# A Mamba scan's spread products: one full-array product for each channel group instead of pairs of 32-row products

## The chip, the cores and the metric

The kernel runs on one core of a Trainium2 chip. The metric is the device time of one execution in microseconds, as the median of several runs. Engines have short names below: PE is TensorE (matrix products), DVE is VectorE, ACT is ScalarE, POOL is GpSimd and SP is SyncE, which issues transfers. Everything is float32, and every matrix product is issued as two passes, so that the profile counts two matmul records for one product in the code.

## The reference, cut to what matters

Two layers work on x of shape (4, 1024, 128): attention and a mixture of eight experts, then a Mamba block and a second mixture of experts. The change lies in the selective scan of the Mamba block:

```python
def _selective_scan(u, A, B_sel, C_sel, delta):
    deltaA = jnp.exp(delta[..., None, None] * A[None, None])
    deltaB_u = delta[..., None, None] * B_sel[:, :, None, :] * u[..., None]
    def step(h, inp):
        a_t, bu_t, c_t = inp
        h = a_t * h + bu_t
        y_t = jnp.einsum('bdn,bn->bd', h, c_t)
        return (h, y_t)
...
xz = x @ W_in
x_main, z = jnp.split(xz, 2, axis=-1)
... # depthwise convolution over 4 tokens
x_conv = jax.nn.silu(jnp.swapaxes(x_conv, 1, 2))
proj = x_conv @ W_xproj
B_sel = proj[..., :D_STATE]
C_sel = proj[..., D_STATE:2 * D_STATE]
delta = jax.nn.softplus(proj[..., -1])
A = -jnp.exp(log_A)
y = _selective_scan(x_conv, A, B_sel, C_sel, delta)
y = y + x_conv * D_param[None, None, :]
y = y * jax.nn.silu(z)
return y @ W_out
```

There are 128 channels (d), 16 states (n) for each, 4 sequences (b) and 1024 tokens in each.

## The kernel before

**Stages.** Attention with the first mixture of experts beside it fills the execution up to about 1425 us. Then the Mamba block runs, sequence by sequence, up to about 1965 us, with the last expert blocks of the first layer (`Blocks`, `first_blocks`), the preparation of the next sequence (`scan_inputs`) and the routing of the sequence before (`dispatch`) beside it. The second mixture of experts ends the program (`slots_steps`, `collect`, `last_experts`).

**The layout of the scan.** The 128 x 16 pairs of channel and state don't fit on 128 partitions, so the scan goes over 16 groups (NCH) of 8 channels; in a group the partitions hold 8 channels by 16 states. Tokens go in two halves of 512 (g). So there are 4 x 2 x 16 = 128 steps, taken two at a time by `scan(pair, g, ...)`.

**One step of the scan.** `du` (delta times the convolved input) lies with one channel on each partition. A product with a matrix of ones and zeros, `spread`, copies each of 8 rows of `du` to 16 partitions, into a PSUM bank `pu` (L909; one of four banks, `pu0` to `pu3`, in turn). DVE multiplies `pu` by B (L911). ACT makes `da`, the exponential of delta times A (L913). DVE runs the recurrence along the tokens (`tensor_tensor_scan`, L915), giving `h`; ACT keeps its last column as `carry` (L917); POOL multiplies by C (L919), giving `hc`. After four steps `collected` sums the 16 states of each channel by products with `gather`, each 32 columns wide and placed side by side in the array, into `py`, which the product of `skip` (D times the identity) has started.

**How `spread` is made and used.** `four` (L791) is the identity folded to 32 columns: every block of 32 partitions holds its own 32 x 32 identity. POOL widens each column 16 times (L793), so that `spread[:, v]` spreads the v-th 8 channels of each block of 32 rows. A product for group c takes only the 32 rows that hold its channels, `rows = 32 * (c // 4)`, and `spread[rows, c % 4]`. The two groups of a pair are chosen in the main loop so that their rows are in neighbouring blocks of 32. `next_to` keeps the second product of a pair right behind the first in the order on TensorE.

**Order.** Program order is written out by hand with generators (`Beside`, `take`): after each pair some steps of the work beside the scan are issued. A scheduler then orders the instructions of each engine; each engine works through its own list in order. A wait on one instruction holds up all that stand behind it on that engine.

**Other names that the prediction uses.** `p` are the products of `scan_inputs` (convolution with `conv_in`, `m_in`, `m_B`, `m_C`, and `ones` for the step sizes `dt`); `pd`, `pl`, `pin`, `fpl`, `fpin` and `pall` are products of few columns in the step sizes and the routing; `pw` is the output projection, whose gated result `wide_gated` (L936) POOL adds to x (L939); `tp` and `ftp` are transposes by the identity; `pf` are products of the first layer's experts; `hs`, `slots_in`, `xe` and `g_in` belong to the routing of the second layer; L195 is the last residual addition of attention.

Of the kernel before, what the change touches and what calls it, by code (L numbers as in the profile page):

```python
# [11 lines left out]
F32 = mybir.dt.float32  # L12
I32 = mybir.dt.int32
AF = mybir.ActivationFunctionType
ALU = mybir.AluOpType
AX = mybir.AxisListType
PSUM = bass.MemoryType.PSUM

P = 128
B, S, D = 4, 1024, 128  # L20
# [7 lines left out]
NST = 16  # L28
NCH = 16
# [15 lines left out]
def mm(nc, out, lhsT, rhs, start=True, stop=True):  # L45
    return nc.tensor.matmul(out, lhsT, rhs, start=start, stop=stop)  # L46
# [3 lines left out]
def adaln_two_layers(ctx: ExitStack, tc: tile.TileContext, I: dict, out: bass.AP):  # L50
    nc = tc.nc
# [16 lines left out]
    ident = cst.tile([P, P], F32, name="ident")  # L68
# [128 lines left out]
    def next_to(first, make):  # L197

        if first:
            make()  # L200
            return
        with tc.high_priority():
            tc.keep_in_program_order(make())
# [259 lines left out]
    with ExitStack() as es:  # L463
# [19 lines left out]
        for j in range(4):  # L483
            rows = slice(j * QG, (j + 1) * QG)
            nc.gpsimd.tensor_copy(mask[rows, MW - QG :], causal[rows, rows])

        for slots in f_in + xd + [g_in]:
            flat = slots.rearrange("(p r) d -> p (r d)", p=P)
            for at in range(0, flat.shape[1], 512):
                n = min(512, flat.shape[1] - at)  # L490
# [29 lines left out]
        def values(hT):  # L520

            v = ab.tile([P, TB, 4 * HD], F32, tag="v", bufs=1, name="v")
            for t in range(TB):
                pv = ps_m.tile([P, 4 * HD], F32, tag="m", name="pv")
                mm(nc, pv, hT[:, t * P : (t + 1) * P], wv)
                nc.scalar.copy(v[:, t, :], pv)
            return v
# [133 lines left out]
        for at, (b, c) in enumerate(stages):  # L661
            q, k = made
            if c == 0:
                v = values(hT)
# [72 lines left out]
    with ExitStack() as es:  # L737
        mc = es.enter_context(tc.tile_pool(name="mc", bufs=1))
        db = es.enter_context(tc.tile_pool(name="db", bufs=2))
        mb_scope = es.enter_context(ExitStack())  # L740
        mb = mb_scope.enter_context(tc.tile_pool(name="mb", bufs=2))
        fw_scope = ExitStack()
        fb = fw_scope.enter_context(tc.tile_pool(name="fb", bufs=2, side="right"))
        ps_u = es.enter_context(tc.tile_pool(name="ps_u", bufs=1, space=PSUM))
# [29 lines left out]
        def first_blocks(b):  # L774
# [12 lines left out]
        nc.scalar.activation(negA, m_logA, AF.Exp)  # L787
        nc.vector.tensor_scalar(negA, negA, -1.0, None, ALU.mult)

        four = mc.tile([P, 32], F32, name="four")  # L790
        nc.vector.tensor_reduce(four, ident.rearrange("p (r d) -> p d r", d=32), AX.X, ALU.add)  # L791
        spread = mc.tile([P, 4, 8, NST], F32, name="spread")
        nc.gpsimd.tensor_copy(  # L793
            spread.rearrange("p v a n -> p (v a) n"), four.unsqueeze(2).to_broadcast([P, 32, NST])
        )
        group = mc.tile([P, 8], F32, name="group")
        nc.vector.tensor_reduce(group, ident.rearrange("p (a n) -> p a n", n=NST), AX.X, ALU.add)
        gather = mc.tile([P, 4, 32], F32, name="gather")
# [10 lines left out]
        def wide(tag, bufs=2, cols=S):  # L809
            return mb.tile([P, cols], F32, tag=tag, name=tag, bufs=bufs)  # L810
# [85 lines left out]
        turn = itertools.count()  # L896

        def scan(pair, g, carry, dt, du, bb, cc):


            tok = slice(g * 512, (g + 1) * 512)
            hcs, pus = [], []
            for _ in pair:
                pus.append(ps_u.tile([P, 512], F32, tag=f"pu{next(turn) % 4}", name="pu"))
            for n in range(2):
                c = pair[n]
                rows = slice(32 * (c // 4), 32 * (c // 4) + 32)
                lhsT = spread[rows, c % 4].rearrange("p a n -> p (a n)")
                next_to(n == 0, lambda: mm(nc, pus[n], lhsT, du[rows, tok]))  # L909
            for c, pu in zip(pair, pus):  # L910
                nc.vector.tensor_mul(pu, pu, bb[:, tok])  # L911
                da = wide("da", 3, 512)
                nc.scalar.activation(da, dt[:, tok], AF.Exp, scale=negA[:, c : c + 1])  # L913
                h = wide("h", 3, 512)
                nc.vector.tensor_tensor_scan(h, da, pu, carry[:, c : c + 1] if g else 0.0, ALU.mult, ALU.add)  # L915
                if g == 0:
                    nc.scalar.copy(carry[:, c : c + 1], h[:, 511:512])  # L917
                hcs.append(wide("hc", 10, 512))
                nc.gpsimd.tensor_mul(hcs[-1], h, cc[:, tok])  # L919
            return hcs  # L920
# [8 lines left out]
        def scan_output(b, g, py, sz):  # L929

            y = wide("yh", 1, 512)
            nc.vector.tensor_mul(y, py, sz[:, g * 512 : (g + 1) * 512])
            pw = ps_m.tile([P, 4, D], F32, tag="d", name="pw")
            for q in range(4):
                mm(nc, pw[:, q], y[:, q * P : (q + 1) * P], m_out)
            u = mb.tile([P, 4, D], F32, tag="wide_gated", name="wide_gated")  # L936
            nc.vector.tensor_mul(u, pw, gate_a1[:, b : b + 1, :].to_broadcast([P, 4, D]))
            xt = x[:, b * TB + 4 * g : b * TB + 4 * g + 4, :]
            nc.gpsimd.tensor_add(xt, xt, u)  # L939
# [249 lines left out]
        for b in range(B):  # L1189
# [17 lines left out]
            for m in range(NCH):  # L1207

                g, n = divmod(m, NCH // 2)
                hcs += scan([4 * (2 * n % 4 + r) + n // 2 for r in range(2)], g, carry, *scanned)  # L1210
                for f in among:
                    if m >= f.at:
# [17 lines left out]
                if n == NCH // 2 - 1:  # L1230

                    def late(b=b, g=g, hcs=hcs, py=py, sz=sz):
                        collected(3, hcs, py)
                        scan_output(b, g, py, sz)

                    hcs = []
# [105 lines left out]
        _, placei, w = sent[0]  # L1342
# [74 lines left out]
```

## Time and profile before

| what | value |
|---|---|
| median of 3 runs | 2198.94 us (2198.32 to 2199.18) |
| profiled execution | 2186.78 us, span 2185.1 us |
| mean granted clock of TensorE, whole span | 0.878 |
| the same from 1470 to 1965 us | 0.66 |
| PE busy from 1470 to 1965 us | 384.80 of 495 us |
| DVE busy from 1470 to 1965 us | 361.39 of 495 us |
| products `pu` (two passes each) | 128, busy 146.5 us |
| scans `h` on DVE, 512 tokens each | 128, median 1.211 (first half) or 1.270 us (second) |

A page of the profile gives each engine's busy time, the span in 40 slices with tenths of busy time (and, in the row PEclk, tenths of the full clock that TensorE was granted), the chain of waits that ended last, and groups of instructions. A row of a stretch of time reads: the stretch, its length, then busy us and number of instructions of PE, of PE's weight loads, of DVE, ACT and POOL, then the granted clock, the share of the transfer engines and GB/s. A row of a wait reads: who waited, for whom, us in total, how many times, the longest. A row of the timeline reads: start, length, engine, line, operation, what it writes from what, shapes (for a product: rows * columns of the stationary operand, then the moving operand), and how many such records were merged.

### The profile page before, as it was taken

The page shows a single profiled execution, that of the slowest core. Times are in us where ns is not written, and L with a number is a line of the kernel's source. Part 1 is how long each engine was busy: PE and PEld are TensorE (multiplying, and loading weights), DVE is VectorE, ACT ScalarE, POOL GpSimd, SP SyncE. Part 2 cuts the span into 40 slices and gives each one's busy share as a digit, 9 for nine tenths or more (in the row PEclk, how much of TensorE's full clock was granted, in tenths as well). Part 3 has the DMA queues.
Part 4 walks back from the last instruction along what each step waited for, and adds up shares of the span by engine and source line. Part 5 has one row for each costly group of instructions (what it writes and reads, how often), then busy time and mean ns, then how long its engine had stood idle before and what let it go on. Part 6 is the DMA issues. An engine that isn't in the chain of part 4 may idle for free. (4 is left out here: it accounts for less than half of the span.)

```text
span 2185.1 us, 29044 instructions
## 1 busy us (share of the span) xinstructions
PE 1832.8 (84%) x8957; PEld 972.7 (45%) x8957; DVE 1321.1 (60%) x4001; ACT 939.5 (43%) x2067; POOL 993.6 (45%) x1277
## 2 busy tenths in 40 slices
PE   5399999998999898999988999959698858859784
PEld 3144444454555354455444456523245423227563
DVE  5446566565667755667675566537587785861323
ACT  1145454653454464445374455433564334323221
POOL 1334444346333736523644633244563666571524
PEclk9699999999999998999999999965687757559897
DMA  6300101002222101222200212110121220012425
GB/s 224 126 1 20 30 1 38 12 19 55 72 64 76 48 1 44 77 66 64 77 6 29 69 58 75 35 34 0 35 71 51 75 99 20 1 51 82 131 72 153
DMA packets 103756, 123.59 MB, mean 57 GB/s; under 512 B 15024, under 2 KB 68656, under 8 KB 103600
## 3 DMA queue, kind: packets, MB, share of 16 engines
q1 hardware_dynamic: 84256, 99.01, 15.4%
q0 software_dynamic: 8192, 16.74, 2.5%
q10 hardware_dynamic: 11152, 5.97, 0.9%
q8 instruction: 71, 1.16, 0.2%
q14 instruction: 85, 0.70, 0.1%
HBM read 67.85 MB, written 32.90 MB: 46 GB/s over the span
## 5 line engine op out<-in xcount | busy, mean ns | idle before, releaser
L586 POOL TENSOR_SCALAR pr<-pr,den 128x32 f32<-128x32 f32 (+31 forms) x512 | 353.2, 705 | 301.9 <-DVE den L583 295.8
L580 ACT ACTIVATE pr<-pr,nb 128x32 f32<-128x32 f32 (+31 forms) x512 | 371.6, 727 | 196.9 <-DVE nb L567 193.6
L595 PE MATMUL pt<-ident,pr 128*128 128x128 f32 x2304 | 341.9, 283 | 47.6 <-POOL pr L586 38.1
L46 PE MATMUL sc<-k,q 64*128 64x512 f32 (+14 forms) x1536 | 329.4, 520 | 43.8 <-DVE nb L567 25.3
L595 PEld LDWEIGHTS pt<-ident,pr 128*128 128x128 f32 x2304 | 253.2, 142 | 243.6 <-POOL pr L586 77.4
L46 PE MATMUL po<-pT,v 128*64 128x512 f32 x1152 | 344.7, 621 | 1.8 <-DVE pT L599 1.8
L597 ACT COPY pT<-pt 128x512 f32<-128x512 f32 x288 | 167.7, 582 | 354.9 <-PE pt L595 301.9
L567 DVE CUSTOM_DVE_ANT_0 pr<-sc,mask 128x512 f32<-128x512 f32 (+15 forms) x512 | 272.9, 559 | 73.5 <-PE sc L46 63.9
L599 DVE COPY pT<-pt 128x512 f32<-128x512 f32 x288 | 198.3, 688 | 167.2 <-PE pt L595 154.1
L919 POOL TENSOR_TENSOR hc<-h,cc 128x512 f32<-128x512 f32 x128 | 161.0, 1272 | 127.7 <-DVE h L915 60.2
L46 PEld LDWEIGHTS sc<-k,q 64*128 64x128 f32 x1536 | 122.4, 191 | 198.7 <-DVE nb L567 93.7
L46 PE MATMUL pu<-du,spread 32*128 32x512 f32 x256 | 146.5, 953 | 34.0 <-DVE h L915 30.1
L684 POOL MEMSET pr<- 128x288 f32 x128 | 42.3, 339 | 264.4 <-PE pt L595 260.3
L567 DVE CUSTOM_DVE_ANT_0 pr<-sc,mask,nb 128x416 f32<-128x416 f32 (+15 forms) x256 | 119.9, 496 | 7.0 <-PE sc L46 5.8
L913 ACT ACTIVATE da<-dt,negA 128x512 f32<-128x512 f32 x128 | 91.0, 718 | 75.8 <-DVE h L915 75.5
L911 DVE TENSOR_TENSOR pu<-pu,bb 128x512 f32<-128x512 f32 x128 | 85.9, 686 | 39.9 <-PE pu L46 39.4
L1302 POOL DMA_INDIRECT y<-slots_out,slot x56 | 57.9, 1033 | 108.4 <-PE ph L46 50.7
L46 PEld LDWEIGHTS po<-pT,v 128*64 128x64 f32 x1152 | 69.3, 135 | 84.1 <-issue 42.0
L503 DVE TENSOR_TENSOR rot_w<-proj,sin_sb 128x512 f32<-128x512 f32 x80 | 55.0, 688 | 77.5 <-PE proj L46 44.4
L46 PEld LDWEIGHTS pf<-fxT,fw 128*128 128x128 f32 x552 | 73.5, 202 | 53.6 <-DVE fye L450 15.5
L580 ACT ACTIVATION_READ_ACCUMULATOR pr<-pr,nb 128x1 f32 x512 | 96.3, 188 | 0.0
L545 POOL TENSOR_TENSOR q<-rot_u,rot_v 128x512 f32<-128x512 f32 x64 | 81.3, 1271 | 32.8 <-DMA rot_v<-rot_w 29.1
(273 smaller groups left out, 2714.3 us busy)
## 6 DMA issues: line engine op xcount, KB each, us to landing
fw<-in_f_w SPq DMA_DIRECT2D x92, 320.0 KB, 3.0
rot_v<-rot_w SPq DMA_DIRECT2D x320, 64.0 KB, 2.0
gw<-in_g_w SPq DMA_DIRECT2D x15, 512.0 KB, 5.2
fxe<-blocks_in SPq DMA_DIRECT2D x28, 192.0 KB, 2.6
blocks_out<-fye SPq DMA_DIRECT2D x28, 192.0 KB, 3.0
blocks_in<-mask SPq DMA_DIRECT2D x20, 256.0 KB, 5.2
slots_in<-mask SPq DMA_DIRECT2D x16, 256.0 KB, 4.7
g_w<-in_g_w SPq DMA_DIRECT2D x8, 512.0 KB, 6.4
```

Source lines behind the costliest of these rows:

```text
L46: return nc.tensor.matmul(out, lhsT, rhs, start=start, stop=stop)
L545: nc.gpsimd.tensor_add(to, u.rearrange("p (n q) -> p n q", q=QG), v.rearrange("p (n q) -> p n q", q=QG))
L567: nc.vector.tensor_tensor_reduce(out=pr[hp][:, g, lo:hi], in0=sc[:, hp, : hi - lo], in1=mask[:, MW - hi + lo :] if hi == nk else mask[:, : ...
L580: nc.scalar.activation(p, p, AF.Exp, bias=nb[:, last, hp : hp + 1], scale=-1.0, accum_out=den[:, hp : hp + 1])
L586: nc.gpsimd.tensor_scalar(p, p, den[:, hp : hp + 1], 1.0, ALU.mult, ALU.mult)
L595: next_to(hp == 0 and g == 0, lambda: nc.tensor.transpose(to, p, ident))
L597: nc.scalar.copy(pT[:, hp, :], pt)
L599: nc.vector.tensor_copy(pT[:, hp, :], pt)
L911: nc.vector.tensor_mul(pu, pu, bb[:, tok])
L913: nc.scalar.activation(da, dt[:, tok], AF.Exp, scale=negA[:, c : c + 1])
L919: nc.gpsimd.tensor_mul(hcs[-1], h, cc[:, tok])
L1302: nc.gpsimd.indirect_dma_start(out=y, out_offset=None, in_=yd[k][:, :], in_offset=bass.IndirectOffsetOnAxis(ap=slot[:, k, t : t + 1], axis=0),
```

## The change

`spread` gets one full 128-row operand for each of the 16 groups: POOL widens the whole identity, 128 columns to 128 x 16, so that `spread[:, c]` has ones where a row's channel belongs to group c and zeros in all other rows. The reduction into `four` goes. In `scan` each product takes all 128 rows of `du` and the operand of its group; the pairs' `next_to` goes, and a bank is taken right before its product. `spread` takes 8 KB of a partition where it took 2; `wide_gated` gets one buffer where it had two.

```diff
-        four = mc.tile([P, 32], F32, name="four")
-        nc.vector.tensor_reduce(four, ident.rearrange("p (r d) -> p d r", d=32), AX.X, ALU.add)
-        spread = mc.tile([P, 4, 8, NST], F32, name="spread")
+        spread = mc.tile([P, NCH, 8, NST], F32, name="spread")
         nc.gpsimd.tensor_copy(
-            spread.rearrange("p v a n -> p (v a) n"), four.unsqueeze(2).to_broadcast([P, 32, NST])
+            spread.rearrange("p c a n -> p (c a) n"), ident.unsqueeze(2).to_broadcast([P, P, NST])
         )
...
-            for _ in pair:
-                pus.append(ps_u.tile([P, 512], F32, tag=f"pu{next(turn) % 4}", name="pu"))
-            for n in range(2):
-                c = pair[n]
-                rows = slice(32 * (c // 4), 32 * (c // 4) + 32)
-                lhsT = spread[rows, c % 4].rearrange("p a n -> p (a n)")
-                next_to(n == 0, lambda: mm(nc, pus[n], lhsT, du[rows, tok]))
+            for c in pair:
+                pu = ps_u.tile([P, 512], F32, tag=f"pu{next(turn) % 4}", name="pu")
+                mm(nc, pu, spread[:, c].rearrange("p a n -> p (a n)"), du[:, tok])
+                pus.append(pu)
...
-            u = mb.tile([P, 4, D], F32, tag="wide_gated", name="wide_gated")
+            u = mb.tile([P, 4, D], F32, tag="wide_gated", bufs=1, name="wide_gated")
```

## The prediction

> **What bounds the kernel now.** I read the page first, then the tile query on `pu`, the waits of VectorE in the stretch where the scan runs, the PE timeline, and last that stretch cut into pieces of 3.41 us, because the granted clock turned out to be constant inside such pieces.
>
> ```profile
> span 2185.1 us, 29044 instructions
> PE 1832.8 (84%) x8957; PEld 972.7 (45%) x8957; DVE 1321.1 (60%) x4001; ACT 939.5 (43%) x2067; POOL 993.6 (45%) x1277
> PEclk9699999999999998999999999965687757559897
> L46 PE MATMUL pu<-du,spread x256: 587/1056/1218, 1470.9 to 1925.2; 32*128 32x512 f32 x128
> 1470.00:1965.00 495.00, 384.80 (x1250) 170.00 (x1249) 361.39 (x781) 199.82 (x378) 292.77 (x249) 0.66 0.14 44
> DVE pu L911 <- PE pu L46: 39.4, 17, 10.2
> DVE r_m L222 <- PE pl L46: 19.4, 5, 6.0
> DVE pos L975 <- PE pin L46: 11.0, 4, 4.9
> DVE wide_gated L937 <- PE pw L46: 8.9, 6, 3.7
> DVE yh L932 <- PE py L46: 5.5, 1, 5.5
> ```
>
> The clock row falls from 9 to between 5 and 8 in slices 27 to 36 (54.6 us each): that is the scan. All products that the change touches lie between 1470.9 and 1926 us. In 1470:1965 the columns are length, then busy time of PE, weight loads, DVE, ACT, POOL, then clock: PE works 384.8 of 495 us at a mean clock of 0.66, DVE 361.4. DVE is idle for 495 - 361.4 = 133.6 us, and the five waits shown, all on products of TensorE, make 84.2 us of that. So the stretch is held by two engines in turn: DVE, which has 128 multiplications (0.687 us) and 128 scans (1.21 or 1.27), 247 us in all, and a TensorE at half clock. The last 220 us (experts of the second layer) and the first 1425 hold no product of this kind.
>
> ```profile
> 1472.87 2.08 PE L46 MATMUL p<-xc,m_B_sb 128*128 128x512 f32 x2
> 1474.88 2.08 PE L46 MATMUL pu<-du,spread 32*128 32x512 f32 x4
> 1623.15 1.13 PE L46 MATMUL pu<-du,spread 32*128 32x512 f32 x4
> 1628.05 1.88 PE L46 MATMUL p<-hT,conv_in 128*128 128x512 f32 x4
> ```
>
> A product is two passes. At half clock a product on all 128 rows takes 2.08 us (x2), and a pair of 32-row products takes the same 2.08 (x4): the two run side by side. At full clock the pair takes 1.13 and two full-row products 1.88.
>
> ```profile
> 1472.62:1476.03 3.41, 3.41 (x8) 1.00 (x6) 2.92 (x4) 1.49 (x5) 0.00 (x0) 0.50 0.00 0
> 1510.17:1513.58 3.41, 3.41 (x10) 0.46 (x10) 3.39 (x7) 1.28 (x2) 1.99 (x2) 0.50 0.00 0
> 1513.58:1516.99 3.41, 3.25 (x8) 0.99 (x4) 3.41 (x11) 0.72 (x1) 1.67 (x2) 0.50 0.00 0
> 1540.89:1544.30 3.41, 3.41 (x5) 1.35 (x4) 3.41 (x11) 2.25 (x3) 3.24 (x3) 0.50 0.06 22
> 1544.30:1547.71 3.41, 3.41 (x16) 0.81 (x15) 0.23 (x3) 2.08 (x3) 3.22 (x4) 1.00 0.06 19
> 1776.41:1779.82 3.41, 3.41 (x14) 1.09 (x12) 3.41 (x1) 0.00 (x0) 3.41 (x2) 0.50 0.06 19
> 1779.82:1783.23 3.41, 0.46 (x4) 0.00 (x0) 3.41 (x2) 0.00 (x0) 3.24 (x2) 1.00 0.00 0
> ```
>
> PE is busy without a gap in nearly all of them, yet the clock comes up only after 1540.89 and 1776.41. I count passes by the part of the array that they use: 1 for 128 rows by 512 columns, a quarter for 32 rows, for a 32-column product of `gather` or for a 128-column transpose. 1540.89 held 4 passes of `conv_in`; 1776.41 one pass of `skip`, four transposes and eight of `gather`, also 4. 1472.62 held two full passes and four of `pu`: 3, and the clock stayed at 0.50. 1510.17 held eight of `gather` and one of `pu`: 2.25, and it stayed. So what raises the clock is array used, not time busy; about three and a half full passes in a piece are needed, and a 32-row product counts for little. Weights of ones and zeros (`gather`, the identity) count like others.
>
> **The change, part by part.** *Products.* 128 products of 32 rows, in pairs, become 128 of 128 rows, each alone. By start times, 80 of the 256 passes now run side by side at half clock (20 pairs), 80 at half clock without a partner, 80 in pairs at full clock (20 pairs) and 16 alone. A pass that has no partner costs the same with 32 rows or 128. Side by side at half clock, a pair of 2.08 becomes 4.0 if the clock stays, but 1.88 if it comes up; at full clock 1.13 becomes 1.88. With the full clock throughout, 256 passes at 0.47 are 120 us against the present 146.5; with the half clock throughout, 256.
>
> *The clock.* Each pair now brings 4 passes to the count, not 1. DVE needs 2 x (0.687 + 1.24) = 3.9 us for a pair, so at its pace a piece gets 4 x 3.41 / 3.9 = 3.5 passes of `pu`, and nearly 0.9 from `gather`: enough. Where PE has a backlog at half clock the piece fills with 4 full passes and the clock comes up a piece later. Where DVE does routing and norms between scans the count falls below three and the clock drops: at 1728 and at 1851 three passes in a piece were not enough to hold it, at 1612 they were. So I expect the mean clock of 1470:1965 to go from 0.66 to about 0.85, not to 1.
>
> [...]
>
> *What it is worth.* Of the 84.2 us that DVE waits for products, I take 70% to fall into pieces that turn from half to full clock (from 0.66 to 0.85 is 56% of the way to 1; the waits lie where PE is loaded, so more), and halve those: 84.2 x 0.7 x 0.5 = 29. The bounds are 0 (clock unchanged) and 42 (all halved). The preparation of the next batch (convolution, step sizes, `du`) waits for TensorE through ScalarE and POOL: the row chain holds about 28 us of such `p` products after 1470 at half clock, but many start from rest, where the clock is low anyway. I take 5, bounds 0 and 14.
>
> *Against it.* Pairs that are now at full clock: the chain has 7.9 us of them, and 1.13 becoming 1.88 adds 5.2; take 5.5, bounds 0 (hidden by DVE) and 20 x 0.75 = 15. The order of instructions changes too: ScalarE gets 58 table loads for 52, six more of 1.283 us, 7.7 in all; ACT is busy 200 of 495 us, so most are hidden; take 3, bounds 0 and 7.7. The copy that builds `spread` writes 2048 columns for 512; 512 took 0.618 us, so 2.5, now ahead of the last residual addition on POOL: +1, bounds 0 and 1.9. The reduction into `four` goes: DVE, less than 0.3 us, not on the path. One buffer for `wide_gated`: its next use comes half a batch later, some 40 us, and POOL reads it within a few us: 0; if that cover were gone, 1.27 us eight times. On POOL `du` of the third batch now stands behind three row scatters that stood behind it; they take 1.0 us and 0.3 between: +1, bounds 0 (they are done before `dt` is there) and 3.9. On SP one load of `g_in` moves behind one of `slots_in`, and one store of `blocks_out` behind the reading of an expert's number; both are used tens of us later: 0. Otherwise the queues differ only in how the products, scans and scatters interleave, and I put no price on that.
>
> *Sum.* -29 - 5 + 5.5 + 3 + 1 + 1 = -23.5 us. The profiled execution took 2186.78 us (1.7 of them around its span of 2185.1): 2163.3. The runs shown have the median 2198.94, 12.2 above it, so the forecast is 2175.
>
> **The rivals.** *The clock stays where it was; slower.* The place is the scan, the price the loss of pairing: 20 pairs x 1.92 at half clock and 20 x 0.75 at full clock are 53 us more of PE. `pu` is on the chain for 73 of its 146.5 busy us, so half of that, 27, plus 5 of the side terms: 2231. It decides once fewer than about a third of the pieces that are now at half clock come up. For it: the count is from few pieces, and products of nearly empty weights might count less than I think. Against: 1776.41, where `gather` and the identity are most of the work. [...]
>
> *DVE closes the gap.* What PE gives, DVE, POOL (hc, 1.27 us x128) and ScalarE take back, since each runs in a fixed order: from 1795 to 1815 DVE is already full. Then the gain meets the 10.5 us of costs and the time stays within 0.2%: 2199.
>
> *More than forecast.* The clock holds at full; DVE's waits halve (42), preparation gains 14, side terms are hidden: -56 or more, 2143. For it: PE would then need about 250 us of 495. Against: 49 us of DVE's idle time are not ended by PE at all, and remain.
>
> *The change does not do what it says.* The products' forms will be 128*128 in the build; only their effect on the clock is open. No separate chance.
>
> **How the numbers follow.** Forecast 0.55; more than forecast 0.15; no difference 0.09; slower by the clock 0.16; slower in a small way, by order and table loads, 0.05. What counts as no change is 0.2%, 4.4 us. Faster 0.70, same 0.09, slower 0.21. The likeliest case alone reaches from 2155 to 2190; the range for 8 in 10 goes from 2142 (full clock, nothing lost) to 2222 (most of the slower rival).
>
> **What would show it.** Right: `pu` as 128*128 with a median near 0.5 us a pass, clock of 0.8 or more over the scan, the wait of `pu` L911 on PE well under 39.4, span near 2160. Wrong: passes of about 1.0 us and a clock near 0.6 with PE busy without gaps (the slower rival); or a high clock with the same length, DVE's idle time now ended by POOL or ScalarE (the gap closed). The first 1425 us should be the same to 1 us.

## The result and the profile after

| | before | after |
|---|---|---|
| median, 4 runs each | 2199.06 us (2198.32 to 2199.58) | 2176.47 us (2173.37 to 2180.41) |
| ratio | 1 | 0.9883, 95% interval 0.9864 to 0.9902 |
| a second series (label e6_after_again below) | 2184.14 us, 17 runs | 2158.22 us, 6 runs, ratio 0.9873 (0.9847 to 0.9900) |
| profiled execution | 2186.78 us | 2174.76 us |

The change is faster by some 1.2%, 23 to 26 us. The profiled execution of before is not one of its four runs in the first series (they took 2198 us or more), so the two profiled executions of the table give a smaller difference, 12.0 us. First the page of the changed kernel, its three lines that answer to those shown before:

```profile
span 2173.1 us, 29054 instructions
PE 1790.6 (82%) x8957; PEld 967.9 (45%) x8957; DVE 1322.2 (61%) x4000; ACT 948.1 (44%) x2073; POOL 997.5 (46%) x1277
PEclk9699999999999999999999999988799877869786
```

PE is busy 42.2 us less (1832.8 to 1790.6) with the same 8957 matmul passes, and the clock row lies between 6 and 9 in slices 27 to 36, the scan, where it was between 5 and 8. The tile query on `pu` in the same kernel:

```profile
L46 PE MATMUL pu<-du,spread x256: 590/593/1222, 1474.6 to 1892.1; 128*128 128x512 f32 x128
```

The median pass now takes 593 ns where it took 1056, although it has four times the rows; 219 of the 256 passes take under 0.7 us, where 92 did before. The scan ends 33 us earlier in this profile (last product at 1892.1, not 1925.2). The scan's stretch, in the window view, ends earlier too, so it is given here over 465 us:

```profile
1470.00:1935.00 465.00, 335.86 (x1253) 160.00 (x1251) 362.43 (x775) 211.59 (x390) 296.18 (x249) 0.83 0.15 47
```

The same work of DVE, 362.4 us against 361.4, fits into 465 us where it took 495: DVE's idle time went from 133.6 to 102.6 us, and the clock from 0.66 to 0.83. The waits of DVE in that stretch:

```profile
DVE pu L906 <- PE pu L46: 23.3, 8, 10.1
DVE r_m L222 <- PE pl L46: 14.5, 4, 8.2
DVE wide_gated L932 <- PE pw L46: 10.1, 6, 3.9
DVE yh L927 <- PE py L46: 8.4, 2, 6.9
```

With 1.1 us for `pos` on `pin`, the five waits that made 84.2 us before make 57.4. The wait on `pu` fell by 16.1, that on `pin` by 9.9, that on `pl` by 4.9; those on `pw` and `py` grew by 1.2 and 2.9.

**What is not the change.** From its first product of the last experts (`ph`) to its end the profile above took 236.4 us; before took 218.8. The second series has a profile of the same program. The window view of the three, from the first `ph` to the end (before, after, after again):

```profile
1966.31:2185.09 218.78, 160.91 (x955) 123.81 (x955) 58.63 (x163) 47.19 (x79) 72.89 (x72) 0.87 0.36 109
```

```profile
1936.65:2173.06 236.41, 165.55 (x955) 127.20 (x955) 58.62 (x165) 46.81 (x79) 72.15 (x72) 0.85 0.34 101
```

```profile
1937.93:2156.56 218.63, 160.97 (x955) 123.73 (x955) 58.64 (x165) 47.13 (x79) 72.56 (x72) 0.86 0.36 109
```

All three have 955 matmul passes and nearly the same busy times there; only the first profile of after is longer, by 17.8 us. Its chain of waits has two pieces there that belong to no instruction of the kernel:

```profile
2033.19 10.21 another core or an unknown queue
2113.06 20.22 another core or an unknown queue
```

The chain of the second profile has no such piece. So these 18 us are not a cost of the change: the same program runs without them. Whether they belong to this one execution or to the whole first series is open, since its four runs of after are alike (2173 to 2180 us), and before, too, took 15 us longer in it than in the second series. A reading of where the change's gain went must be taken from the stages before 1937 us. From the end of the first `du` (when the scan can start) to the first `ph`: 495.5 us before, 462.1 and 468.6 after in the two profiles.

### The profile page after: what moved, and what is told of

It is laid out like the page before. It is cut to its first block, busy times and chain, and to the rows that moved or that the text cites. A ratio compares the mean times of both kernels' runs of the same rounds, so it can differ in the third digit from the quotient of the medians.

```text
span 2173.1 us, 29054 instructions
## 1 busy us (share of the span) xinstructions
PE 1790.6 (82%) x8957; PEld 967.9 (45%) x8957; DVE 1322.2 (61%) x4000; ACT 948.1 (44%) x2073; POOL 997.5 (46%) x1277
## 5 line engine op out<-in xcount | busy, mean ns | idle before, releaser
L46 PE MATMUL pu<-du,spread 128*128 128x512 f32 x256 | 147.0, 679 | 48.8 <-DVE h L910 41.7
L46 PEld LDWEIGHTS pu<-du,spread 128*128 128x128 f32 x256 | 45.8, 208 | 117.8 <-DVE h L910 70.5
```

## The experiments

All ratios are to the kernel before on the same chip. "Stretch" is the time from the end of the first `du` to the first `ph` of that label's profile, "clock" is the mean over the window 1475 to 1930 us, "wait on `pu`" is DVE's wait for TensorE. In e7 another 9.5 us of the same multiplication are put down to ACT. The expectations give some times in us at the level of the first series, where before took 2199 us; in the series below before took 2184 to 2185, so those are better read as differences.

| label | products | order form | ratio (95%) | median us | clock | wait on `pu` us | stretch us |
|---|---|---|---|---|---|---|---|
| before | 32 rows, pairs | before | 1 | 2183.77 / 2184.14 / 2184.89 | 0.67 | 39.4 | 495.5 |
| e1_order | 32 rows, pairs | after | 1.0021 (1.0005 to 1.0038) | 2186.49 | 0.66 | 40.1 | 498.0 |
| e2_rows | 128 rows | before | 0.9912 (0.9886 to 0.9938) | 2164.26 | 0.81 | 29.4 | 474.5 |
| e7_rows_again | 128 rows | before | 0.9917 (0.9892 to 0.9943) | 2167.47 | 0.82 | 22.9 | 475.4 |
| e6_after_again | 128 rows | after | 0.9873 (0.9847 to 0.9900) | 2158.22 | 0.81 | 26.8 | 468.6 |
| e3_half | 64 rows, pairs | before | 0.9978 (0.9961 to 0.9994) | 2178.53 | 0.74 | 35.4 | 483.7 |
| e4_useless | 32 rows, pairs, and one unused of 128 rows for each pair | before | 0.9975 (0.9957 to 0.9992) | 2178.35 | 0.81 | 32.3 | 482.7 |
| e5_useless32 | the same, the unused one of 32 rows | before | 1.0102 (1.0071 to 1.0132) | 2206.36 | 0.67 | 62.5 | 512.4 |
| e8_after_useless | after, and one unused of 128 rows for each pair | after | 0.9916 (0.9884 to 0.9948) | 2168.63 | 0.89 | 31.4 | 479.4 |
| e9_order_useless | 32 rows, and one unused of 128 rows for each pair | after | 1.0015 (0.9995 to 1.0035) | 2188.29 | 0.78 | 43.0 | 496.9 |

### e1_order and e2_rows: the two halves of the change, each alone

e1 takes the order form of the changed kernel (a bank taken right before its product, no `next_to`) and keeps the 32-row products. e2 takes the 128-row products and keeps the order form of before, so that the products stand on TensorE in the order of before.

```diff
 # e1_order, against before
-            for _ in pair:
-                pus.append(ps_u.tile([P, 512], F32, tag=f"pu{next(turn) % 4}", name="pu"))
-            for n in range(2):
-                c = pair[n]
+            for c in pair:
+                pu = ps_u.tile([P, 512], F32, tag=f"pu{next(turn) % 4}", name="pu")
                 rows = slice(32 * (c // 4), 32 * (c // 4) + 32)
-                lhsT = spread[rows, c % 4].rearrange("p a n -> p (a n)")
-                next_to(n == 0, lambda: mm(nc, pus[n], lhsT, du[rows, tok]))
+                mm(nc, pu, spread[rows, c % 4].rearrange("p a n -> p (a n)"), du[rows, tok])
+                pus.append(pu)
```

```diff
 # e2_rows, against after
-            for c in pair:
-                pu = ps_u.tile([P, 512], F32, tag=f"pu{next(turn) % 4}", name="pu")
-                mm(nc, pu, spread[:, c].rearrange("p a n -> p (a n)"), du[:, tok])
-                pus.append(pu)
+            for _ in pair:
+                pus.append(ps_u.tile([P, 512], F32, tag=f"pu{next(turn) % 4}", name="pu"))
+            for n in range(2):
+                c = pair[n]
+                lhsT = spread[:, c].rearrange("p a n -> p (a n)")
+                next_to(n == 0, lambda: mm(nc, pus[n], lhsT, du[:, tok]))
```

> The kernel before with its 32-row products, but the two of a pair asked for as in the changed kernel (bank taken right before its product, no rule that keeps the second behind the first). TensorE's order is then that of the changed kernel, and ScalarE has 58 table loads. Theory clock (a product counts for the clock by the share of the array that it uses): nothing raises the clock, mean of the scan stretch 0.62 to 0.70, pairs that are pulled apart cost up to 1 us each, time 2195 to 2220 us. Rival order (the gain is from the new order, not from the rows): about 2176 us.

> The changed kernel with its 128-row products, but the two of a pair asked for as in the kernel before (both banks first, the second product kept right behind the first). TensorE's order is then that of the kernel before, and ScalarE has 52 table loads. Theory clock: mean clock of the scan stretch 0.80 or more, and six table loads fewer than in the changed kernel, so 2165 to 2180 us. Rival order: about 2199 us or, since each pair takes longer, more.

The order form alone leaves the clock where it was (0.66) and costs 4.6 us (0.0021 of 2184), interval 1 to 8. The rows alone bring the clock to 0.81 and 19 us. In the traces every engine starts its instructions from 1450 us on in the same order in before and e2, and again in e1 and the changed kernel, so each of these pairs differs in the rows alone (and in what goes with them: the work that prepares `spread`, and the one buffer of `wide_gated`). So here the clock (0.67 to 0.81) and most of the gain come from the rows. The two halves do not add up to the whole: +4.6 and -19 are some -14, and the change brings -26 to -28. e6 and e7 come back to it.

### e4_useless and e5_useless32: rows without any other difference

Both take the kernel before and add a product ahead of each pair, into the bank that the pair's first product then overwrites; its result is unused. The two have the same instructions, and DVE, ACT and POOL run theirs in the same order; they differ in the rows of the added product alone.

```diff
 # e4_useless, against before
+            mm(nc, pus[0], ones, du[:, tok])
 # e5_useless32, against before
+            rows = slice(32 * (pair[0] // 4), 32 * (pair[0] // 4) + 32)
+            mm(nc, pus[0], ones[rows], du[rows, tok])
```

> The kernel before, pairs of 32 rows kept, with one more 128-row product (ones times du) before each pair, into the bank of the pair's first product, which then overwrites it: 64 products whose result is not used. Theory clock: each pair brings 3 full passes to the count instead of 1, the mean clock of the scan stretch rises to 0.80 or more, and although TensorE has 64 x 0.94 = 60 us more work at full clock the time falls below that of before, 2170 to 2195 us. Rival (more work on an engine that is busy 385 of 495 us is simply slower): 64 x 1 to 2 us, half of them on the path, 2230 to 2265 us.

> As e4_useless, but the added product takes only the 32 rows of the pair's first product. The order of the instructions is the same as in e4_useless, and a product alone takes as long with 32 rows as with 128. Theory clock: the added product counts a quarter of that of e4_useless, the clock stays at 0.60 to 0.70 and the added work is paid, 2225 to 2270 us, 40 us or more above e4_useless. Rival (what counts is how long TensorE is busy, not the rows): the same clock and time as e4_useless.

The window view over the first 12 pieces of the clock in the scan, first e4, then e5:

```profile
1471.16:1512.12 40.96, 36.94 (x123) 11.86 (x122) 36.42 (x50) 17.55 (x42) 21.39 (x17) 0.88 0.00 0
```

```profile
1471.33:1512.29 40.96, 40.61 (x92) 14.99 (x94) 22.32 (x26) 15.20 (x37) 15.15 (x13) 0.50 0.00 1
```

In e5 PE is busy 40.61 of 40.96 us at a clock of 0.50 throughout; in e4 it is busy less, 36.94 us, at 0.88, with 123 matmul passes where e5 has 92. DVE gets 36.4 us of work through in e4 and 22.3 in e5. Over the whole run e4 is 28 us faster than e5. That is the way I expected, but less than the 40 us or more that I had put on it, and e5 stayed under its range. e4 is also 5 us faster than before, with 64 products more, but there the order differs too: the added products make the scheduler order the engines' lists anew, so only e4 against e5 is free of it. This is the clearest result of the study: between these two the rows of the added product, not the time that TensorE was busy, made the clock 0.81 or 0.67 over the scan. A pass costs the same with either number of rows, as the expectation of e5 took it, where the clock is the same: in before, at half clock, the median pass takes 1056 ns with 32 rows and 1061 ns with 128.

### e3_half: the step between

Pairs of 64-row products side by side: `spread` folds the identity to 64 columns, a pair takes groups of the two halves, and `collected` takes the results in the changed order.

```diff
-                rows = slice(32 * (c // 4), 32 * (c // 4) + 32)
-                lhsT = spread[rows, c % 4].rearrange("p a n -> p (a n)")
+                rows = slice(64 * (c // 8), 64 * (c // 8) + 64)
+                lhsT = spread[rows, c % 8].rearrange("p a n -> p (a n)")
...
-                hcs += scan([4 * (2 * n % 4 + r) + n // 2 for r in range(2)], g, carry, *scanned)
+                hcs += scan([4 * (n % 2 + 2 * r) + n // 2 for r in range(2)], g, carry, *scanned)
```

> Products of 64 rows in pairs: spread is folded to 64 columns, the two groups of a pair are taken from different halves of the rows, so that they run side by side and use the whole array, and the order on TensorE is that of the kernel before. A pair counts 2 full passes for the clock (128-row products: 4, 32-row pairs: 1) and costs 1.1 us at full clock (1.88 and 1.13). Theory clock: the mean clock of the scan stretch lies between those of the kernel before and of the changed one, 0.70 to 0.80, and the time between them or, as the pair is cheaper, a little under the changed kernel: ratio to before 0.980 to 0.997. Rival (only products without partner tiles raise the clock): 0.62 to 0.70 and the time of before. Rival (only time busy matters): the time of before.

Two 64-row products side by side use as many rows of the array as one full product. The median pass of e3 takes 693 ns; the median one of 32 rows in e4 takes 692. Clock (0.74), wait on `pu` (35.4) and time (0.9978) all lie between before and e2; the ratio is a little above the 0.980 to 0.997 that I expected. The order on all engines is that of before, and pairs too raise the clock here (0.67 to 0.74), so it is not the pairing as such that holds it down. Keeping the packing and filling the array at once was still worth less, a ratio of 0.9978, than the two full products of e2 one after the other, 0.9912 at a clock of 0.81.

### e6_after_again and e7_rows_again: what the order form is worth

The changed kernel and e2_rows again, on one chip.

> The changed kernel once more, without an edit, for a second profile beside the others. In its first profile the last part, from the first product of the second layer's experts (ph) to the end, took 236 us, where the kernel before took 219 and e2_rows, with 128-row products too, 217. Theory clock says nothing of this part, which holds no spread product: if the 17 us belong to that one execution, the last part takes 216 to 221 us now and the ratio to before is 0.985 to 0.990. Rival (the changed order on ScalarE and SP costs the 17 us each time): 230 us or more again.

> e2_rows once more, on the same chip as e6_after_again, to tell the price of the new order alone: 128-row products in both, 52 table loads here and 58 there. If the six loads cost what the prediction took, this kernel is 3 us faster than the changed one, 0 to 8; if the new order is a gain in itself, it is slower.

The changed kernel is 9.3 us faster than the same products in the order of before (six runs each, 2150.16 to 2160.47 against 2162.43 to 2169.72, and no overlap; the ratios' intervals overlap a little, 0.9900 and 0.9892). So the order form, which costs 4.6 us with 32 rows, gains 9 with 128. The largest gain is in the third sequence. From its `du` to the next one, in the window view, first e7, then e6:

```profile
1681.37:1834.24 152.87, 104.14 (x392) 52.16 (x392) 110.08 (x246) 59.01 (x115) 102.94 (x88) 0.79 0.20 68
```

```profile
1684.45:1822.17 137.72, 98.37 (x369) 49.21 (x369) 103.57 (x233) 62.34 (x115) 101.80 (x86) 0.79 0.19 67
```

At the same clock of 0.79 this stage is 15.2 us shorter: 6.5 us less work of DVE falls into it, and 8.6 us less idle time. Part of that is given back in the neighbouring sequences. The same cut for all four (from the end of a sequence's `du` to the next, the last to the first `ph`), in us:

| label | rows, order form | first | second | third | fourth |
|---|---|---|---|---|---|
| before | 32, before | 114.2 | 106.2 | 157.6 | 117.4 |
| e1_order | 32, after | 116.2 | 120.0 | 140.8 | 121.0 |
| e7_rows_again | 128, before | 106.7 | 103.3 | 152.9 | 112.5 |
| e6_after_again | 128, after | 106.0 | 109.1 | 137.7 | 115.8 |

The order form shortens the third sequence by 15 to 17 us with either kind of product, and lengthens the second and the fourth. With 32 rows the second grows by 13.8 us, at a clock of 0.74, and that eats the gain; with 128 rows it grows by 5.8. That is where the two differ most; why the second grows so much more with 32 rows was not isolated.

### e8_after_useless and e9_order_useless: is the rest of the clock worth anything?

e8 adds the unused 128-row product of e4 to the changed kernel, e9 adds it to e1_order.

```diff
             for c in pair:
                 pu = ps_u.tile([P, 512], F32, tag=f"pu{next(turn) % 4}", name="pu")
+                if c == pair[0]:
+                    mm(nc, pu, ones, du[:, tok])
```

> The changed kernel with one more product of 128 rows ahead of each pair, whose result is unused (the next product writes over it): 64 products, two passes each, 60 us of TensorE at full clock. If what is left of the gap to the full clock (0.83 over the scan) still costs time, a pair now gives 6 passes to the count, the clock of the scan goes above 0.88, the wait of VectorE on pu goes below 20 us, and the kernel is a few us faster than the changed one (ratio to before 0.983). If the waits that are left stand at products of few columns, which the added passes do not reach, the clock rises and the time does not: the added passes cost up to 10 us in DVE's waits on pu, ratio 0.988 to 0.993. I expect the second.

> 32-row products in the order form of the changed kernel (as e1_order, ratio 1.0021), with one more product of 128 rows ahead of each pair, whose result is unused. If the full array is what raises the clock, it goes from 0.66 to about 0.8 over the scan and the kernel ends clearly below e1_order. If the order form of the changed kernel gains by itself once the clock is up (as the 9 us between e7_rows_again and e6_after_again suggest), the ratio is near 0.992; if it does not, near that of e4_useless, 0.9975.

The tile query of e8 and its window from 1475 to 1930 us:

```profile
L46 PE MATMUL pu<-du,ones x128: 590/592/1222, 1471.6 to 1903.2; 128*128 128x512 f32 x128
```

```profile
1475.00:1930.00 455.00, 363.49 (x1347) 173.40 (x1345) 364.33 (x729) 200.17 (x368) 281.03 (x237) 0.89 0.14 45
```

e8 came out as I expected of it: the clock rises once more, from 0.81 to 0.89, and by the medians the kernel is 9 us slower than the changed one (0.9916 against 0.9873, on two chips, with intervals that overlap from 0.9884 to 0.9900). So a gain from the higher clock does not show; DVE's wait on `pu`, ahead of whose pair the added passes stand, is 31.4 us, not 26.8. The added products also changed the order of all engines, so the clock's own share of this result is not isolated.

e9 was a miss. Its clock is at 0.78, near e4's 0.81, and yet it is as slow as e1 (1.0015 against e4's 0.9975). So neither "the order form gains once the clock is up" nor "the order form does nothing" holds. Each of these two edits makes the scheduler put the engines' lists in another order than e1 or e4 has, and the sign of what that does, 5 to 10 us, was predicted by nothing that I tried. e8 against e9 is free of that: from 1450 us on their engines work in the same order, and on one chip the 128-row kernel is 19.7 us faster (2168.63 against 2188.29), at a clock of 0.89 for 0.78.

## Why the prediction was right, and where its terms were not

The sum was -23.5 us; the medians of the two series differ by 22.6 and 25.9. The mechanism holds: with 128 rows the clock rises (0.66 to 0.83), and DVE waits less (84.2 to 57.4 us). That the sum is so near is in part luck, because two things were off in opposite directions.

**The clock by use of the array: shown.** Forecast 0.85, measured 0.83 and 0.81; e4 against e5 leaves only the rows as a cause. That the clock is constant inside pieces of 3.41 us shows in the clock records of the traces: of before and after, 26 and 33 stretches of one clock start between 1470 and 1965 us, and each lasts a whole number of pieces of 3.413 us, to 1 ns. Over the scan stretch of all eleven profiles I sorted the pieces of 3.41 us by the passes that started in them, each weighted by the part of the array that it uses:

```
passes in the piece      at half clock: came up      at full clock: fell
under 2.5                    0 of 373                   133 of 141
2.5 to 3                     7 of  84                    16 of  21
3 to 3.5                    60 of 122                    15 of  48
3.5 to 4                    30 of  35                     0 of  33
4 and more                  67 of  67                     0 of 558
```

The forecast had "about three and a half" for the rise; in these profiles half of the pieces with 3 to 3.5 passes came up (60 of 122), and at full clock 16 of 21 with 2.5 to 3 fell, against 15 of 48 with 3 to 3.5. Among the 373 pieces under 2.5 passes there are 128 in which PE was busy without a gap, and none came up. In before PE was busy 19.12 of the 21 us from 1499 to 1520 at a clock of 0.50. Those pieces and e5 (40.61 of 40.96 us at 0.50) show that busy time alone did not bring the clock up here.

Single pieces of the changed kernel, in the window view:

```profile
1472.92:1476.33 3.41, 3.06 (x4) 0.84 (x3) 0.00 (x0) 2.63 (x7) 1.67 (x1) 0.50 0.01 2
1476.33:1479.74 3.41, 3.41 (x9) 1.44 (x8) 2.98 (x4) 1.81 (x5) 0.00 (x0) 1.00 0.00 0
...
1493.40:1496.81 3.41, 3.11 (x25) 2.20 (x26) 3.41 (x5) 2.90 (x8) 2.51 (x3) 1.00 0.00 0
1496.81:1500.22 3.41, 3.41 (x5) 1.36 (x5) 2.52 (x6) 1.61 (x5) 2.54 (x3) 0.50 0.00 0
1500.22:1503.63 3.41, 3.41 (x14) 1.06 (x14) 3.41 (x7) 1.13 (x4) 1.38 (x2) 1.00 0.00 0
```

The scan's first piece (1472.92) holds one pass of `p` and two of `pu`, three in all, at half clock, and the next is at full clock; before, the same place held two full passes and four of 32 rows, also three by this count, and stayed low: at 3 to 3.5 the count does not decide, as the table shows (60 of 122). The piece at 1493.40 holds 25 matmuls, but 16 of them are `fpl`, 8 columns each:

```profile
1494.77 1.95 PE L46 MATMUL fpl<-gate_wT_sb,fhT 128*128 128x8 f32 x16 [0.21 <-ACT fhT L186]
1496.57 5.38 PE L46 MATMUL pu<-du,spread 128*128 128x512 f32 x8
```

The count there is 3.25 (eight passes of `gather` make 2, one of `pu` 1, the sixteen a quarter); the next piece, 1496.81, is at 0.50, four passes of `pu` start in it, and the one after it is at 1.00. The timeline puts that burst of eight passes at 5.38 us. But pieces like 1493.40, filled with products that stream few columns, are the smaller part of what is left. Of the scan's pieces at half clock, before had 28 with PE busy for nine tenths or more and under 2.5 passes; after has 2. Of the 45 pieces still at half clock in after, PE is idle for more than a tenth in 30.

**The gain of DVE's waits (-29): 26.8 in the first profile,** 84.2 to 57.4, and 22.0 in the second. But these profiles have the new order too. With the order of before the waits of e2 are:

```profile
DVE pu L908 <- PE pu L46: 29.4, 10, 10.2
DVE r_m L222 <- PE pl L46: 14.7, 5, 5.9
DVE wide_gated L934 <- PE pw L46: 8.2, 4, 3.9
DVE yh L929 <- PE py L46: 7.9, 2, 6.4
DVE pos L972 <- PE pin L46: 4.3, 2, 3.2
```

The five make 64.5 there and 66.8 in e7 (its 9.5 on ACT included), 17 to 20 us less than before; the stretch shrinks by 21.0 and 20.1 us and the time by 19 and 18 (0.0088 and 0.0083 of 2184). The terms that belong to the rows, -29 - 5 + 5.5, promised 28.5. So in the order in which it was worked out, this sum was worth about two thirds of its forecast. I had taken 70% of the waits to lie where the clock comes up, and half of those to go; the wait on `pu` did fall (39.4 to 29.4 and 32.4), but those on products of few columns or of others' passes fell less or rose: in after `pl` went from 19.4 to 14.5, `pw` from 8.9 to 10.1 and `py` from 5.5 to 8.4.

**The order of instructions (+3 for table loads, "no price" on the rest): the step that failed.** The sum added a cost of the order to a gain of the rows as if each had one price. They don't. With 32 rows the order costs 4.6 us (1 to 8), near the term of 3; with 128 rows it gains 9. Seen the other way, the rows are worth 18 to 19 us in the order of before and 30 to 32 in the new one (ratio 1.0021 for e1 against 0.9883 and 0.9873 for the changed kernel), which is close to the 28.5. So some 11 to 14 us belong to neither half alone, and which one they are booked to is a choice. The 58 table loads are there in e1 and in e6, so they don't explain it. The prediction left exactly this out, at nothing, and it happened to fill what the rows did not bring in the old order; why the two act together stays open.

**The small terms.** The copy into `spread` took 1.89 us (1432.68 to 1434.57), forecast 2.5. From the end of attention's last `po` product (weights times values) to the end of the first `du` takes 44.2 us in both profiles of after and 47.9 in before, so no cost of it shows. The `du` of the third sequence starts at 1681.40, where its `dt` was ready at 1677.84: two scatters and one `hc` stand between. It is held by 3.5 us, forecast 1 with the bound 3.9; before, it started 0.1 us after its `dt`. The loss on pairs that were at full clock (+5.5) and the preparation (-5) could not be taken apart from the waits.

**"The first 1425 us should be the same to 1 us": too strict.** Attention's last `po` product ends between 1421.5 and 1430.4 us in these eleven profiles; the second profile of the changed kernel has it 5.3 us before the first. A bound for such a control must come from more than one profile of the same kernel.

**The rivals.** "The clock stays" would need passes near 1.0 us; they took 0.593. "DVE closes the gap" did not happen as told: DVE idles 102.6 us of 465 still. The point of the slower rival, though, is real in e5: 32-row work added at half clock cost 22 us.

## What to carry to other kernels

In these runs TensorE's clock went with how much of the array worked in each piece of 3.41 us, not only with how long it was busy: with four or more full passes of 128x128 by 512 columns 67 of 67 pieces at half clock came up and 0 of 558 at full clock fell, and under 2.5 passes 0 of 373 came up. Where a profile shows PE busy without gaps at a granted clock of 0.5, products that use more rows, even rows of zeros, are worth a run before packing them; here they took the clock of the scan from 0.67 to 0.81 and 19 us off the time (e2). A higher clock was not a gain by itself: e8 raised it further, from 0.81 to 0.89, with more work and another order, and was no faster (0.9916 against 0.9873). And where an edit lets a scheduler reorder four engines, leave some 10 us on a kernel of this size for the order alone, of either sign, and separate it from the edit by two runs, one with the order without the edit and one with the edit without the order: here they did not add up to the whole, and either alone would have misled.

## What the runs showed that was not expected

**Work for nothing made a kernel faster.** With e4's 64 unused products the time is 0.0025 lower (interval 0.0008 to 0.0043), at a clock of 0.81 for 0.67. How much of that is the order, which the products changed too, is open; the 28 us between e4 and e5 are not.

**A short operation of DVE that lasts as long as POOL's work beside it.** In e7 (and in before) one residual addition of 128x128, 0.34 us elsewhere, is recorded with 7.52 us. The timeline of DVE, then of POOL, in the same stretch of e7:

```profile
1765.25 7.52 DVE L278 SCALAR_TENSOR_TENSOR x<-fy,f_w,x 128x128 f32<-128x128 f32 x1
```

```profile
1765.67 2.35 POOL L947 TENSOR_TENSOR hs<-hx,row_scale 128x1024 f32<-128x1024 f32 x1
1767.97 2.35 POOL L1009 TENSOR_TENSOR x<-x,gate_bias 128x1024 f32<-128x1024 f32 x1
1770.28 2.33 POOL L948 TENSOR_TENSOR hs<-hs,row_shift 128x1024 f32<-128x1024 f32 x1
```

It ends at 1772.77 with the third of POOL's operations (1772.61). The group of these additions from 1470 to 1960 us, in before and in after:

```profile
L278 DVE SCALAR_TENSOR_TENSOR x<-fy,f_w,x 128x128 f32<-128x128 f32 x16 | 17.1, 1073 | 6.9 <-DMA fy<-blocks_out,f_placei 6.7
```

```profile
L278 DVE SCALAR_TENSOR_TENSOR x<-fy,f_w,x 128x128 f32<-128x128 f32 x16 | 5.4, 340 | 8.7 <-DMA fy<-blocks_out,f_placei 8.6
```

The new order keeps them out of the way, and 11.7 us of DVE's recorded time go from this line; other lines are stretched in the same manner there (a `ln_r` of 128x8 took 4.14 us in e6 beside three `hc` of POOL). Over the scan the time by which DVE's operations exceed the median of their like is some 31 us before and 34 after, so this does not explain the gain of the order. In before the same addition takes 7.53 us and ends at 1783.22, where the third of three such operations of POOL ends at 1783.06. In the first profile of after the stretched one is a `ln_r` of 128x8 with one tensor input, 4.32 us from 1745.52, and three `hc` of POOL beside it end at 1749.80. No run took POOL's work away, so that DVE waited for it is inferred from these times, and by what means was not shown.
